# Two transformer blocks on one core: dues and lists of a hand-written planner (batch 0's output projections, the last pair of maxima, the outputs, the context pieces)

## The chip, the cores and the metric

One core of a Trainium2 chip runs the whole program in one launch. The time is the device's, in microseconds (us). The kernel before takes 2895.8 us (median of 3 runs, 2895.5 to 2897.63).

## What is computed

The reference applies two blocks (layers 0 and 1) to `x`, 4 batches of 512 tokens of width 320, with a context of 4 x 1601 tokens of width 192. Each block has three parts:

```python
h1 = _ln(x, n1_g, n1_b)
x = _attn(h1, h1, q1, k1, v1, o1_w, o1_b, 20) + x        # self
h2 = _ln(x, n2_g, n2_b)
x = _attn(h2, context, q2, k2, v2, o2_w, o2_b, 20) + x   # cross
h3 = _ln(x, n3_g, n3_b)
a, g = split(h3 @ ff_w1 + ff_b1)
x = a * gelu(g) @ ff_w2 + ff_b2 + x                      # feed-forward
```

`_attn` has 20 heads of 16 columns: `softmax(q k^T / 4) v`, then the output projection `@ wo + bo`.

## The kernel before

**Units.** Attention is done in units: one layer, one kind (self or cross), one batch `b` of 4, one group `g` of 4 heads out of 5 groups. A unit goes over its keys in chunks of 128: 4 chunks in self, 13 in cross. The program has 88 units in order: layer 0 self (units 0 to 19, batch by batch), layer 0 cross (20 to 39), four feed-forward units (40 to 43), and the same for layer 1 from unit 44.

**One chunk** (`main`, line 1323). TensorE works in strips of 32 rows, one per head, so four heads run beside each other. `score` (1330) makes for each head three passes into one bank: two of keys by queries (the queries are split in a rounded and a remaining half) and a third that adds the negative row maxima (`nrows`, line 1336). ScalarE takes the exponential (1346), TensorE multiplies by the values one chunk later (1362), ScalarE copies the product out (the first chunk into the unit's output `o`, line 1376; the others into `vo`, 1381), GpSimd adds (1382). `o` is a tile with two buffers (1375), so the unit after next needs the first one's place.

**Row maxima, ahead of time.** The next units' maxima are computed beside the present unit's scores: TensorE repeats the product with the queries as the stationary side (`sps`, 1088 and 1113), VectorE reduces each tile over the keys (1099, 1123). These products come as pairs for two heads each: 8 in a self unit, 26 in a cross unit, in two queues (`pairs[0]`, `pairs[1]`). A chunk has two half rounds, and each has one regular slot, which takes one pair from the queue of its parity; in it the maxima use the strips that the scores leave free. `giver` (line 1635) hands out the pairs of the next two units, and of the first cross unit (called early) from 9 units before. Besides the slots it can order extra rounds of up to two pairs, when pairs are owed by the pace that the remaining rounds ask for, or when a unit's pairs are left in its last slot (lines 1666 to 1671). A unit's pairs can be given 4 rounds after its queries and keys were sent (`at_hand`). When the present unit has two chunks left, `max_reduce` and `max_end` (1157, 1164) finish the next unit's maxima, turn them, and issue four small transfers to `nrows` (1183) from SP; the next unit's third passes wait for these.

**The planner.** Everything else is entered in lists (`chains`, line 396) by `add` with a cost in us of TensorE, a due half round, a condition that must hold (`ready`) and one before which it isn't tried (`soon`). A list is served only from its head. After each chunk `steps` (487) advances the round, adds credit by the pace that all dues ask for, and runs heads in the order of their due rounds (ties by the list's name); at the first one with a cost of 0.1 or more that the credit doesn't cover, it stops. Entries of cost LIGHT (0.01) are limited to one or two per chunk. `carry` (818) then issues the pending moves of queries and keys (888) and the errands.

**The way of an output** (`add_finish`, 1191). After a unit's last values, `turn` sends `o` to memory (1203), two rounds later at the earliest; the tile is then read back with another layout. After a batch's fifth unit: `sums` reads the denominators (1211), `invert` (1215), `save` (1220), `read` loads the first two thirds of the batch's output and of the inverse (1236, 1237), GpSimd multiplies them (`divide`, 1244), `load` fetches the last third a number of rounds later, `divide` again, and `end` (1271) enters eight output projections (`project`, 1255: 24 small products into `ops`, line 1262, and an addition on VectorE, 1269) and `done`, which marks the batch as ready for its next normalisation. `turn`, `invert`, `save`, the divisions and `end` of all units share the list "divide".

**The context, layer 0 only** (`add_turned`, 758). Each batch's context comes in 7 pieces (742, 748). VectorE transposes a piece into one of two `stages` buffers (767), SP saves it to memory (775). Batch 0's pieces are entered when unit 5 starts, with dues 2 rounds apart up to the 22nd round of the unit after; other batches' come in the cross stage, 6 apart. `add_context` reads the saved pieces back into the layout for the products (789), in two steps of four transfers.

**Banks.** The 8 PSUM banks are chosen by `bank` (413), which takes the one that is free first by `expect`, a running estimate of when each engine is done.

**The start** (from line 1695 on). The first units are prepared by an order written out by hand: two batches of `x` and the weights are loaded, units 0 to 3 projected, unit 0's maxima taken. While `start["on"]`, moves go to SP's and ScalarE's queues in turn (886), and so do the `nrows` transfers (1182).

Of the kernel before, what the change touches and what calls it, by code (L numbers as in the profile page):

```python
# [24 lines left out]
NQ = N // P  # L25
# [53 lines left out]
def kernel(ctx: ExitStack, tc: tile.TileContext, x, context, ws, out):  # L79
# [313 lines left out]

    chains = {n: deque() for n in ("divide", "project", "norm", "scale", "context", "early", "proj", "values")}
    clock = {"round": 0, "credit": 0.0, "lights": 0, "tiles": None, "ff": False, "cross": False}
    ALIKE = ("project", "early", "proj", "values")
    LIGHT = 0.01
# [440 lines left out]
    def add_proj(u):  # L840
# [35 lines left out]
        def move(of, pairs, may, gap=0):  # L876

            def f():
                pending[of] -= 1
                if of == "k":  # L880
                    room["sent"] = clock["round"]
                u.moving[of] = clock["round"]
                for to, src in pairs():
                    queue = nc.sync
                    if start["on"]:
                        queue = (nc.sync, nc.scalar)[room["first"] % 2]
                        room["first"] += 1
                    queue.dma_start(out=to.bitcast(F32), in_=src)
                u.open -= 1
                if not u.open:  # L890
                    u.when = -9 if start["on"] else clock["round"]

            pending[of] += 1
            u.moves[of].append((f, may, gap))
            u.moving[of] = clock["round"]
            if (u.i, of, u) not in movers:
                movers.append((u.i, of, u))
# [266 lines left out]
    def max_end(u):  # L1164

        top, high, low = (u.nm[:, :, i, :] for i in range(3))
        nc.vector.tensor_reduce(
            high.bitcast(F32R), top.rearrange("p j (t o) -> p j t o", o=1), AX.X, ALU.max, negate=True
        )
        nc.vector.tensor_reduce(  # L1170
            low, u.nm[:, :, 0:2, :].rearrange("p j e t -> p j t e"), AX.X, ALU.add, negate=True
        )
        turned = two.tile([P, SLOT], F32, tag="turned", name="turned")

        nc.vector.transpose(turned.rearrange("p (j c) -> p j c", j=HG), u.nm[:, :, 1:3, :].rearrange("p j e t -> p j (e t)"))
        busy("dve", 0.6)
        slots = u.rows.bitcast(F32).rearrange("(g s) n -> s g n", s=DH)[0].rearrange("g (t r) -> g t r", t=NQ)

        def rows():
            for i in range(P // SLOT):  # L1180
                part = slice(i * SLOT, (i + 1) * SLOT)
                queue = nc.scalar if start["on"] and i % 2 else nc.sync
                queue.dma_start(out=slots[:, :, part], in_=turned[part, :])

        if u.cross and u.before.cross:
            u.rows_of = rows
            errands.appendleft((clock["round"] + 1, yes, rows))
        else:
            rows()

    def add_finish(u):
# [34 lines left out]
        def read():  # L1226

            held["read"] += 1
            held["open"] += 1
            aT = one.tile([P, 3, N], F32, tag="aT", name="aT")  # L1230
            way, part = o_way[u.b % 2], {}

            def load(k, at, n):
                heads = slice(at // DH, (at + n) // DH)
                part[k] = two.tile([P, N], F32, tag="rT", name="rT")
                dma(out=aT[:n, k, :], in_=way[:DH, heads])
                dma(
                    out=part[k][:n],
                    in_=r_way[u.b % 2][heads].rearrange("(o j) n -> o j n", o=1).to_broadcast([DH, n // DH, N]),
                )  # L1240
                when.append(clock["round"])

            def divide(k, n):
                nc.gpsimd.tensor_tensor(aT[:n, k, :], aT[:n, k, :], part[k][:n], ALU.mult)  # L1244

            for k, at, n in DK[:2]:
                load(k, at, n)
            first, second, third = DK
            add("divide", 0.0, lambda: divide(0, first[2]), r - 20, yes, since(4, 3))
            add("divide", 0.0, lambda: divide(1, second[2]), r - 20)  # L1250
            add("divide", 0.0, lambda: load(*third), r - 20, yes, since(4, 5 if u.l and not u.cross else 7))
            add("divide", 0.0, lambda: divide(2, third[2]), r - 20, yes, since(5, 3))
            add("divide", 0.0, lambda: end(aT), r - 20)

# [15 lines left out]

        def end(aT):
            now = clock["round"]
            for t in range(NQ):
                for part in range(2):
                    add(
                        "project", (0.317,) * 3, lambda t=t, part=part: project(aT, t, part),
                        now + 2 + u.nch * t + u.nch // 2 * part, yes, lambda: clock["round"] >= now + 1,
                    )
            add("project", 0.0, done, now + 2 + u.nch * NQ)

        def done():
            held["open"] -= 1
            after(u)

        r = when[0]
        add("divide", 0.0, turn, r - 20, lambda: u.g or held["written"] < held["read"] + 2, since(0, 2))


    late = []
# [283 lines left out]
    def before(u):  # L1573

        if u.kind == "cross" and u.g == 1 and u.b + 1 < B or u.kind == "self" and u.m == EARLY - 3:
            b = u.b + 1 if u.cross else 0
            if u.l == 0:
                load_context(b, 0)
                load_context(b, 1)
                if u.cross:  # L1580
                    add_turned(b, u.start + 46, 6)
        if u.kind == "self" and u.m == 0 and u.l:
            take_rooms(u.l)
        if u.kind == "cross" and u.m == B * G - 1:
            take_weights()
            loads.extend(load_first(u.l, (0, 1, 3)) + load_ff(u.l)[2])
        if u.kind == "cross" and u.m == B * G - 3:
            take_rests()
            small, rests, _ = load_ff(u.l)
            loads.extend(small + rests)  # L1590
        if u.kind == "cross" and u.m == B * G - 2:
            loads.extend(load_first(u.l, (4, 2)))
        if u.kind == "self" and u.m == EARLY - 1 and u.l == 0:
            add_turned(0, units[u.i + 1].start + 22, 2)
        if u.kind == "self" and u.m == EARLY:

            add_context(0, lambda s: units[u.i - u.m + B * G].own.update(kv=s["cT"]), u.start + 36, yes)
# [37 lines left out]
    def giver(u):  # L1635
# [15 lines left out]
        def give(h, alone=False):  # L1651
# [7 lines left out]
            for v in coming:  # L1659
# [6 lines left out]
                rest = v.start - (7 if alone else 4) - clock["round"]  # L1666
                if rest > 0:
                    most = max(most, (total - rest * (not alone)) / (2 * rest))
                if left(v) and (rest == 1 or alone and rest < 1):
                    urgent = urgent or v  # L1670
                    owed = max(owed, 1.0 if alone and rest > -4 else (left(v) + 1) // 2)
            owed += most * went if total else 0.0
# [54 lines left out]
        run("norm")  # L1727
    max_reduce(first)
    max_end(first)
    at_once(units[2])  # L1730
    second = units[1]
    second.pairs = max_pairs(second)
    round_of(second.pairs[0].popleft()[1] + second.pairs[1].popleft()[1])
    add_proj(units[3])
    run("proj")
    run("proj")
    loads.extend(load_x(2))
    for fs in (load_out(0, "o1_w"), load_x(3), load_cross(0)):
        loads.extend(fs)
# [51 lines left out]
```

## Time and profile before

| | |
|---|---|
| median of 3 runs | 2895.8 us |
| the profiled execution, whole | 2899.26 us |
| its span, first to last instruction | 2897.2 us |
| mean granted TensorE clock | 0.997 |
| VectorE, ScalarE, GpSimd busy | 68%, 67%, 45% |
| HBM read and written | 55.76 and 29.36 MB |

The self stage of layer 0 ends at about 373 us of the span, that of layer 1 goes from about 1487 to 1808 us; between and after them lie the cross stages and, from about 1187 and 2622 us, the feed-forward stages.

How to read it: PE is TensorE's products, PEld its loading of weights, DVE is VectorE, ACT ScalarE, POOL GpSimd, SP SyncE, and a q behind a name is that engine's queue, where it waits or issues transfers. L1088 is line 1088 of the kernel. In the timeline a row has its start, its duration, engine, line, operation, output and inputs, and in brackets the engine's idle time before it with what ended it. In the table of windows a row has the stretch, its length, the busy time and number of instructions of PE, PEld, DVE, ACT and POOL, then the granted TensorE clock as a share of the full one, the busy share of the DMA engines, and GB/s. In the chain of waits a row has its start and duration on the path that ended last. Ends of products are modelled, so a TensorE that is shown as busy may still be held up.

### The profile page before, as it was taken

To read this page: it belongs to the slowest core of one execution; us is meant where nothing else is said; L and a number is where in the kernel's file an instruction comes from. 1 tells how busy PE (TensorE), PEld (TensorE's weight loads), DVE (VectorE), ACT (ScalarE), POOL (GpSimd) and SP (SyncE) were. 2 spreads that over 40 slices of the span, in tenths; PEclk is the share of its full clock that TensorE was granted. 3 is DMA by queue.
4 is the path that set the end of the run, shared out by engine and by line. 5 is a ranking of instruction groups with operands and counts; after the bars stand their busy time and mean duration, and the time that the engine had idled before them with its cause. 6 is when DMAs were issued, how large, how long until landed. Compare 5 with 4: busy or idle time off the path is not lost.

```text
span 2897.2 us, 83291 instructions
## 1 busy us (share of the span) xinstructions
PE 2848.3 (98%) x35028; PEld 1543.2 (53%) x35028; DVE 1972.1 (68%) x3734; ACT 1948.9 (67%) x4033; POOL 1307.5 (45%) x1420
## 2 busy tenths in 40 slices
PE   9999999999999999999999999999999999999999
PEld 5455555555555555355554555555555555544554
DVE  7867888788888888323257678888878878862221
ACT  4867678888888888501138776788888888893000
POOL 5556345555545546211225653455565564551100
PEclk9999999999999999999999999999999999999999
DMA  4444233232232112200123432221221122122000
GB/s 115 118 111 110 66 82 88 57 93 59 57 87 70 48 50 63 85 18 16 38 52 88 106 91 66 71 69 44 54 73 47 44 72 61 45 72 61 23 22 12
DMA packets 163502, 188.59 MB, mean 65 GB/s; under 512 B 62004, under 2 KB 109112, under 8 KB 163128
## 3 DMA queue, kind: packets, MB, share of 16 engines
q1 hardware_dynamic: 161464, 180.38, 24.5%
q8 instruction: 275, 4.51, 0.6%
q10 hardware_dynamic: 1664, 2.89, 0.4%
q14 instruction: 99, 0.81, 0.1%
HBM read 55.76 MB, written 29.36 MB: 29 GB/s over the span
## 4 chain that ended last, share of the span: by engine, by line
PE 87%; DVE 6%; POOL 3%; DMA 2%; issue 1%; ACT 1%; SPq 0%; POOLq 0%; ACTq 0%; DVEq 0%
PE av L1362 22%; PE st L1336 20%; PE fps L1447 10%; PE sps L1088 8%; PE yps L1554 6%; PE vps L1047 5%; PE ops L1262 4%; PE kps L984 3%; DVE nmax L1099 3%; PE qkps L920 3%; PE fps L1507 3%; PE qps L959 2%; DVE pm L1099 2%; PE sps L1113 1%; POOL hturned L630 1%
## 5 line engine op out<-in xcount | busy, mean ns | idle before, releaser
L1346 ACT ACTIVATE pr<-st 128x512 f32<-128x512 f32 (+1 forms) x2720 | 1404.8, 604 | 309.8 <-PE st L1336 278.2
L1099 DVE TENSOR_REDUCE pm<-sps 128x1 f32<-128x512 f32 (+1 forms) x1920 | 1149.1, 661 | 235.1 <-PE sps L1088 230.2
L1382 POOL TENSOR_TENSOR o<-o,vo 128x512 f32<-128x512 f32 x576 | 739.7, 1284 | 916.6 <-ACT vo L1381 899.0
L1088 PE MATMUL sps<-kT,q 32*128 32x512 f32 (+1 forms) x4800 | 858.2, 419 | 3.8 <-ACT halves L936 1.4
L1336 PE MATMUL st<-q,kT 32*128 32x512 f32 (+1 forms) x5120 | 785.3, 419 | 2.7 <-ACT o L1376 2.1
L1362 PE MATMUL av<-pr,vals 128*32 128x512 f32 (+1 forms) x5440 | 735.1, 606 | 30.9 <-ACT pr L1346 5.6
L1336 PEld LDWEIGHTS st<-q,kT 32*128 32x128 f32 (+1 forms) x5120 | 447.6, 180 | 284.1 <-issue 113.4
L1336 PE MATMUL st<-nrows,ones 32*128 32x512 f32 (+1 forms) x2720 | 560.5, 398 | 0.9 <-DMA nrows<-turned 0.7
L1099 DVE TENSOR_REDUCE nmax<-sps 128x1 f32<-128x512 f32 x640 | 397.0, 683 | 115.2 <-PE sps L1088 113.1
L1088 PEld LDWEIGHTS sps<-kT,q 32*128 32x128 f32 x4800 | 429.9, 183 | 54.7 <-ACT pr L1346 11.2
L1381 ACT COPY vo<-av 128x512 f32<-128x512 f32 x576 | 354.0, 615 | 17.4 <-PE av L1362 10.4
L1518 ACT ACTIVATE gl<-fps,b 128x512 f32<-128x512 f32 x80 | 54.7, 687 | 408.9 <-PE fps L1507 299.1
L1447 PE MATMUL fps<-hT,w 128*128 128x512 f32 x640 | 283.1, 597 | 0.0
L1362 PEld LDWEIGHTS av<-pr,vals 128*32 128x32 f32 (+1 forms) x5440 | 111.1, 108 | 304.2 <-DVE pm L1099 186.7
L1336 PEld LDWEIGHTS st<-nrows,ones 32*128 32x128 f32 (+1 forms) x2720 | 262.9, 180 | 10.1 <-issue 2.0
L1519 DVE SCALAR_TENSOR_TENSOR hid<-fps,b,gl 128x512 f32<-128x512 f32 x80 | 59.7, 748 | 249.2 <-ACT gl L1518 247.1
L1447 PEld LDWEIGHTS fps<-hT,w 128*128 128x128 f32 x640 | 119.3, 190 | 155.0 <-issue 151.6
L1554 PE MATMUL yps<-w,hid 128*128 128x320 f32 x640 | 175.7, 435 | 0.0
L1554 PEld LDWEIGHTS yps<-w,hid 128*128 128x128 f32 x640 | 120.6, 190 | 56.2 <-ACT gl L1518 5.3
L1262 PEld LDWEIGHTS ops<-wo,aT 112*32 112x32 f32 (+1 forms) x3072 | 98.9, 110 | 66.0 <-issue 34.9
L1262 PE MATMUL ops<-wo,aT 112*32 112x160 f32 (+1 forms) x3072 | 125.7, 301 | 2.6 <-POOL aT L1244 2.6
L1123 DVE TENSOR_REDUCE pm<-sps 128x4 f32<-128x508 f32 x160 | 99.0, 682 | 39.8 <-PE sps L1113 38.8
(89 smaller groups left out, 2458.2 us busy)
## 6 DMA issues: line engine op xcount, KB each, us to landing
kT<-stages SPq DMA_DIRECT2D x80, 400.5 KB
oway<-o SPq DMA_DIRECT2D x80, 256.0 KB
q<-halves SPq DMA_DIRECT2D x80, 256.0 KB
q<-halves SPq DMA_DIRECT2D x27, 512.0 KB
kT<-halves SPq DMA_DIRECT2D x40, 256.0 KB
aT<-oway SPq DMA_DIRECT2D x32, 224.0 KB
rT<-rway SPq DMA_DIRECT2D x32, 224.0 KB
hT<-hturned SPq DMA_DIRECT2D x96, 64.0 KB
```

The costliest lines, as they stand in the source:

```text
L1047: nc.tensor.matmul(ps[f : f + m, :w], lhsT=u.kvT[:n, k, at + f : at + f + m], rhs=wv[:n, k, h0 * DH : h1 * DH], start=(k == 0), stop=(k == ...
L1088: nc.tensor.matmul(own[0][:, :w], lhsT=u.queries(slice(j * SLOT, (j + 1) * SLOT), e, t), rhs=u.kT[j * SLOT : (j + 1) * SLOT, u.k0 + at : u ...
L1099: nc.vector.tensor_reduce(to, own[0][:, :w], AX.X, ALU.max)
L1123: nc.vector.tensor_reduce(u.pm[:, :, j, ns - 1], ps[:, : NQ * w].rearrange("p (t w) -> p t w", w=w)[:, :, :n], AX.X, ALU.max,)
L1262: nc.tensor.matmul(ps[f : f + m, : D // 2], lhsT=aT[:n, k, f * NQ + t * SLOT : f * NQ + t * SLOT + m], rhs=wo[:n, k, cols], start=(k == 0) ...
L1336: nc.tensor.matmul(own[0][:r, :], lhsT=ones[rows, :r] if e == 2 else u.keys(rows, c), rhs=u.rows[rows, :] if e == 2 else u.queries(rows, e ...
L1346: nc.scalar.activation(p[:r], own[0][:r], AF.Exp)
L1362: nc.tensor.matmul(ps[j * SLOT : (j + 1) * SLOT, :], lhsT=columns_of[:r, head : head + SLOT], rhs=pr.pop((c, j))[:r, :], start=True, stop= ...
L1381: nc.scalar.copy(vo, ps)
L1382: nc.gpsimd.tensor_tensor(u.o, u.o, vo, ALU.add)
L1447: nc.tensor.matmul(ps, lhsT=w1[:, k, i * FF + c * P : i * FF + (c + 1) * P], rhs=natural(u.hT[:, k]), start=start, stop=stop,)
L1554: nc.tensor.matmul(ps[:, :D], lhsT=hid[c][:, t * P : (t + 1) * P], rhs=w2[:, c, :], start=(c == 0), stop=(c == NHC - 1),)
```

## The change

- The list "way" is new and holds the `turn` of each unit; "divide" keeps the rest.
- The last third of a batch's output is loaded 5 rounds after the second in both layers' self stages, where layer 0 had 7.
- `end`: the projections of batch 0's self output are due one round apart instead of two (self units have `nch` 4), and `done` accordingly; other batches and the cross stage keep their spacing.
- `giver`: one pair left in a unit's last slot, if it belongs to the queue of that slot, no longer counts as urgent, and so is given in the slot and not in an extra round.
- Batch 0's context pieces are due 3 rounds apart instead of 2, up to the same last round.
- In the start, `at_once(units[2])`, which issues unit 2's moves of queries and keys, stands behind unit 1's first maxima and unit 3's projections; and `expect` counts ScalarE's time for the transfers that it issues.

```diff
-    chains = {n: deque() for n in ("divide", "project", "norm", "scale", "context", "early", "proj", "values")}
+    chains = {n: deque() for n in ("way", "divide", "project", "norm", "scale", "context", "early", "proj", "values")}
...
                         queue = (nc.sync, nc.scalar)[room["first"] % 2]
                         room["first"] += 1
                     queue.dma_start(out=to.bitcast(F32), in_=src)
+                    if queue is nc.scalar:
+                        expect["act"] += 0.6
...
                 queue = nc.scalar if start["on"] and i % 2 else nc.sync
                 queue.dma_start(out=slots[:, :, part], in_=turned[part, :])
+                if queue is nc.scalar:
+                    expect["act"] = max(expect["act"], expect["dve"]) + 1.05
...
-            add("divide", 0.0, lambda: load(*third), r - 20, yes, since(4, 5 if u.l and not u.cross else 7))
+            add("divide", 0.0, lambda: load(*third), r - 20, yes, since(4, 7 if u.cross else 5))
...
         def end(aT):
             now = clock["round"]
+            apart = 1 if not u.cross and u.b == 0 else u.nch // 2
             for t in range(NQ):
                 for part in range(2):
                     add(
                         "project", (0.317,) * 3, lambda t=t, part=part: project(aT, t, part),
-                        now + 2 + u.nch * t + u.nch // 2 * part, yes, lambda: clock["round"] >= now + 1,
+                        now + 2 + u.nch * t + u.nch // 2 * part if u.cross else now + 2 + apart * (2 * t + part), yes, lambda: clock["round"] >= now + 1,
                     )
-            add("project", 0.0, done, now + 2 + u.nch * NQ)
+            add("project", 0.0, done, now + 2 + (u.nch * NQ if u.cross else 2 * NQ * apart))
...
-        add("divide", 0.0, turn, r - 20, lambda: u.g or held["written"] < held["read"] + 2, since(0, 2))
+        add("way", 0.0, turn, r - 20, lambda: u.g or held["written"] < held["read"] + 2, since(0, 2))
...
         if u.kind == "self" and u.m == EARLY - 1 and u.l == 0:
-            add_turned(0, units[u.i + 1].start + 22, 2)
+            add_turned(0, units[u.i + 1].start + 22, 3)
...
-                if left(v) and (rest == 1 or alone and rest < 1):
+                if left(v) > bool(not alone and v.pairs[h % 2]) and (rest == 1 or alone and rest < 1):
                     urgent = urgent or v
...
     max_reduce(first)
     max_end(first)
-    at_once(units[2])
     second = units[1]
     second.pairs = max_pairs(second)
     round_of(second.pairs[0].popleft()[1] + second.pairs[1].popleft()[1])
     add_proj(units[3])
     run("proj")
     run("proj")
+    at_once(units[2])
```

## The prediction

> **What bounds the kernel now.** I read the page first: share of each engine and the chain that ended last.
>
> ```profile
> span 2897.2 us, 83291 instructions
> PE 2848.3 (98%) x35028; PEld 1543.2 (53%) x35028; DVE 1972.1 (68%) x3734; ACT 1948.9 (67%) x4033; POOL 1307.5 (45%) x1420
> ...
> PE 87%; DVE 6%; POOL 3%; DMA 2%; issue 1%; ACT 1%; SPq 0%; POOLq 0%; ACTq 0%; DVEq 0%
> ```
>
> TensorE is the bound: idle for 2897.2 - 2848.3 = 48.9 us. The change alters neither the arithmetic nor the number of matrix products, so it can win only what TensorE loses in waits and in rounds that fill the array badly. Where that is, the two layers tell: their self stages do the same work, but layer 0 also turns the context (L767, L775). I cut both stages by batch (the window view; first column the stretch and its length): batches 1, 2, 3 of layer 0, then of layer 1.
>
> ```profile
> 117.90:201.50 83.60, 77.98 (x1124) 41.48 (x1125) 62.01 (x128) 58.83 (x119) 47.19 (x58) 0.98 0.51 133
> 201.50:290.30 88.80, 85.56 (x1276) 47.49 (x1276) 59.98 (x118) 62.05 (x129) 53.90 (x65) 0.98 0.37 93
> 290.30:373.20 82.90, 81.06 (x1164) 44.56 (x1160) 68.66 (x131) 56.63 (x117) 26.71 (x23) 0.98 0.23 61
> 1563.00:1641.40 78.40, 75.41 (x1125) 41.21 (x1125) 58.35 (x115) 58.74 (x119) 47.06 (x58) 1.00 0.41 107
> 1641.40:1726.40 85.00, 83.42 (x1299) 47.00 (x1291) 59.44 (x118) 62.41 (x129) 53.87 (x65) 1.00 0.38 97
> 1726.40:1808.10 81.70, 79.92 (x1165) 44.60 (x1166) 69.40 (x133) 56.31 (x117) 26.77 (x22) 1.00 0.24 62
> ```
>
> With nearly the same products, layer 0 is longer by 5.2, 3.8 and 1.2 us. Batch 2 first, in the timeline:
>
> ```profile
> 254.92 1.28 POOL L1382 TENSOR_TENSOR o<-o,vo 128x512 f32<-128x512 f32 x1 [0.70 <-ACT vo L1381]
> ...
> 264.90 0.78 SPq L1203 DMA_DIRECT2D oway<-o  x1
> ...
> 271.24 0.57 SPq L1203 DMA_DIRECT2D oway<-o  x1
> ...
> 275.23 0.58 ACT L1376 COPY o<-av 128x512 f32<-128x512 f32 x1 [4.68 <-DMA oway<-o]
> ...
> 275.87 0.73 PE L1336 MATMUL st<-q,kT 32*128 32x512 f32 x3 [2.08 <-ACT o L1376]
> ```
>
> The third unit's output is complete at 256.2 but leaves at 264.90, 6.3 us before the next unit's. What holds it is the list: `turn` is entered in "divide", only the head of a list is ever run, and at the head stand batch 1's divisions, which wait a set number of rounds for their loads. The output buffer has two places, so ScalarE's copy two units on waits 4.68 us for that transfer, and TensorE 2.08 us for ScalarE. In batch 1:
>
> ```profile
> 157.98 0.98 SPq L775 DMA_DIRECT2D ctxT<-stages  x1
> ...
> 163.51 0.60 SPq L775 DMA_DIRECT2D ctxT<-stages  x1
> ...
> 167.42 1.28 POOL L1382 TENSOR_TENSOR o<-o,vo 128x512 f32<-128x512 f32 x1
> ...
> 170.66 0.38 DVE L767 STREAM_TRANSPOSE stages<-stages 128x192 f32<-128x192 f32 x1 [3.25 <-DMA ctxT<-stages]
> ...
> 171.62 2.67 SPq L1183 DMA_DIRECT2D nrows<-turned  x4
> ...
> 172.19 1.94 PE L1362 MATMUL av<-pr,vals 128*32 128x512 f32 x8 [2.44 <-DVE nmax L1099]
> ...
> 179.31 0.60 SPq L1203 DMA_DIRECT2D oway<-o  x1
> ```
>
> The seventh context piece is turned in the buffer of the fifth, whose save left one chunk earlier (163.51). VectorE waits 3.25 us for it, the maxima stand behind it, TensorE stands 2.44 us. After both stops it runs slowly; behind the five engines' busy times stands the granted clock, 0.53 and 0.75:
>
> ```profile
> 172.00:175.00 3.00, 2.81 (x20) 0.99 (x24) 1.93 (x4) 0.58 (x1) 1.19 (x3) 0.53 0.04 8
> 276.00:280.00 4.00, 4.00 (x45) 2.31 (x49) 1.29 (x2) 3.09 (x7) 2.66 (x3) 0.75 0.23 69
> ```
>
> So a stop costs more than its idle time, and the difference between the layers, not the gap, is the price to use.
>
> **Outputs in their own list.** Of the turns, only those are held that fall behind a batch's pending divisions: by the rounds of `add_finish`, one per batch 0, 1 and 2 in each layer. In layer 0 the worst is batch 2's third unit: ready in round 108 (three after its last values), issued in 114 with `end`. Now it goes in 108, soon after 256.2. What is late next there: batch 1's aT loads and the row maxima on SP, which layer 1 has too; its batch 2 takes 85.00. I take **-3.5 us** of the 3.8 (range 0 to -4.7, the copy's wait). Layer 1's held turns were late by two to four rounds and stop nothing in its stretches: nothing.
>
> **Context pieces apart.** The same seven turnings and saves; only their due rounds move, from 56, 58, ... 68 to 49, 52, ... 67. Entries run when at the head and no dearer work is due before them, so the first pieces come up to six rounds sooner and the fifth piece's save takes the place of the row at 157.98, whose successor did not wait. The 3.25 us wait should go. But the last save and the first reading of the saved context move too, from round 70 to 68, and with the output now in 68 instead of 72 three things stand on SP ahead of unit 9's row maxima: an output that waits for GpSimd until 167.42 + 1.28 = 168.7, the save, and four reads that wait for the save to land:
>
> ```profile
> 163.51 7.03 DMA ctxT<-stages
> ...
> 174.34 2.29 DMA ctxT<-stages
> ...
> 331.63 3.01 DMA nrows<-turned
> ```
>
> The reads and, in the window view, the fourth unit of batch 1 in layers 0 and 1:
>
> ```profile
> 176.68 2.53 SPq L789 DMA_DIRECT2D w<-ctxT  x4
> ```
>
> ```profile
> 161.80:179.70 17.90, 14.99 (x187) 6.97 (x179) 11.39 (x23) 11.39 (x24) 15.43 (x24) 0.90 0.51 119
> 1605.90:1621.80 15.90, 14.27 (x213) 7.50 (x213) 10.77 (x21) 11.33 (x24) 15.32 (x24) 1.00 0.55 146
> ```
>
> From 168.7: output 0.6, save landed 2.9 later (2.29, and some more for the output ahead of it), reads 2.53, row maxima 2.67 to issue and 3.01 to land: 168.7 + 0.6 + 2.9 + 2.5 + 2.7 + 3.0 = 180.4. At layer 1's pace TensorE is at unit 9 by 161.8 + 15.9 = 177.7: a new wait of 2.7, and some half microsecond of slow clock behind it. So of 5.2 us I take **-2.0 us**; ends -5.2 (the reads find the save landed) and +2 (7.03 instead of 2.9 for the save, 5.2 - 2.7 - 4.1 - 0.5). The Trainium skill, "DMA: Bandwidth & Descriptors", section "Queues, rings and completion order", says that a transfer's semaphore lands only after every earlier write of the same DMA engines; by it the save always waits for the 256 KB output ahead of it. The rows 7.03 and 2.29 fit that; were it the 7.03 every time, the term would be +2 and the sum -5.0.
>
> **The last pair of maxima.** A pair left over in the last slot was forced into a round of its own. An extra round, in layer 0's batch 3:
>
> ```profile
> 324.66 0.76 PE L1088 MATMUL sps<-kT,q 32*128 32x512 f32 x8
> 325.46 2.42 DVE L1099 TENSOR_REDUCE pm<-sps 128x1 f32<-128x512 f32 x4 [0.24 <-PE sps L1088]
> ```
>
> Four tiles cost 0.76 us where TensorE decides, 2.42 where VectorE does. By the giver's rule the condition holds three times in a layer: at the first unit and the first cross unit it spent a full extra round on the unit after next; before the first cross unit it took that unit's very last pair alone, two tiles. The lone round goes: half of 0.76 to 2.42, so 0.4 to 1.2, I take 0.8, twice: 1.6. The full ones only move: that pair is given in a later slot or extra round, out of places where VectorE is behind; four times 0.3, between 0 and 2.42 - 0.76 = 1.7 each: 1.2. Nothing waits longer: VectorE reduces in order, so `max_reduce` came behind as many reductions before.
>
> **Batch 0's projections.** Eight at one round instead of two:
>
> ```profile
> 291.88 0.82 PE ops L1262 x24
> 1620.37 0.48 PE L1262 MATMUL ops<-wo,aT 96*32 96x160 f32 x8 [1.36 <-POOL aT L1244]
> 182.71 2.12 PE L1262 MATMUL ops<-wo,aT 96*32 96x160 f32 x56 [0.64 <-POOL aT L1244]
> ```
>
> 8 x 0.82 = 6.6 us of TensorE move, none is added. The batch is done some six rounds sooner, and the first cross unit's normalisation, queries and 26 pairs may start so much sooner; its extra rounds spread over longer. Twice 0.35: 0.7 (0 to 2.4, one full extra per layer). With the lone and moved rounds **-3.5 us** (0 to -10). The third aT load two rounds earlier in layer 0 makes it like layer 1, where the first projection meets GpSimd's division: 1.36 instead of 0.64, **+0.7 us** (0 to +1.4).
>
> **The start.**
>
> ```profile
> 36.04 0.60 ACTq L888 DMA_DIRECT2D q<-halves  x1
> 36.77 0.84 ACT L936 ACTIVATE halves<-qkps,scales 128x256 f32<-128x256 f32 x2 [4.13 <-POOL x L623]
> 37.29 0.50 PE L1088 MATMUL sps<-kT,q 32*128 32x512 f32 x2 [1.37 <-ACT halves L936]
> ```
>
> Unit 2's moves now stand behind unit 3's projections, so ScalarE copies before it issues, and the added ScalarE times choose banks that are free. TensorE's 1.37 us goes at most; the row maxima's transfer, issued by 36.0, is late next. **-0.7 us** (0 to -1.4).
>
> **Sum.** -3.5 - 2.0 - 3.5 + 0.7 - 0.7 = -9.0 us. The profiled execution took 2899.3 us (span 2897.2 and 2.1 around it): 2890.3. It is 3.5 above the median 2895.8, the difference of two executions of one program; against the median: **2886.8 us**. The measurement can tell 0.2%, 5.8 us: 2890.0 and 2901.6 are the limits.
>
> **The rivals.** *The stops only change places* (29%): the new wait on SP is 5.5 instead of 2.7 (batch 1 then 5.5 + 0.5 - 5.2 = +0.8), the moved and lone extra rounds yield 1.0, the start 0.5: -3.5 + 0.8 - 1.0 + 0.7 - 0.5 = -3.5, 2892.3. For it: SP is in order and the chain of batch 1 is full of it. In it lies too that the change does not do what it says where the output waits for GpSimd anyway; against that the 254.92 row.
>
> *Slower* (11%): outputs at the head of SP hold up the row maxima.
>
> ```profile
> SPq L1203 <- POOL o L1382: 334.2, 67, 10.6
> ```
>
> SP already stands 334.2 / 67 = 5.0 us on average at an output. Moved forward, six of them (three per layer) come ahead of a unit's row maxima; if each makes those 2.7 us late, as worked out above, and nothing of batches 1 and 2 is won: 6 x 2.7 - 3.5 + 0.7 - 0.7 = +12.7, so 2908.5. It decides once the maxima land after the next unit's third pass, some two chunks after issue. Against it, from the costliest groups (last column: TensorE's idle time before the third passes):
>
> ```profile
> L1336 PE MATMUL st<-nrows,ones 32*128 32x512 f32 (+1 forms) x2720 | 560.5, 398 | 0.9 <-DMA nrows<-turned 0.7
> ```
>
> Today 0.9 us are lost there in 80 units, 74 of which already send their output at once.
>
> *Only the gaps count* (5%): the Trainium skill, "TensorE: Matmul & The Clock Gate", section "Part 1: The HAM clock gate", puts the slow clock behind an idle window of about 3.4 us, longer than either gap. As a mechanism of this kernel: the 2.08 and 2.44 us gaps would be all that a removed stop gives, 2.1 in batch 2 and 2.44 x 2.0 / 5.2 = 0.9 in batch 1: -2.1 - 0.9 - 3.5 + 0.7 - 0.7 = -6.5, 2889.3. The rows with 0.53 and 0.75 speak against it.
>
> **Numbers.** The forecast has 55%, its own range 2880 to 2890. Chances: faster 0.55 + 0.05 = 0.60, same 0.29, slower 0.11. Range: the forecast's far end, -4.7 - 5.2 - 5 (half of the extra rounds' bound) - 0.7, is 2880; upwards it takes in the rival of changed places and its neighbours to 2897.
>
> **What would show it.** Right: batch 2 of layer 0 near 85 us, no copy waiting on the output's transfer; no transposition waiting on a save; the same counts at L1088 and L1099. A wait of TensorE for row maxima of about 2.7 us at the last unit of batch 1 shows the new order on SP; of 5.5, the first rival. Wrong: batches 1 and 2 of layer 0 as long as before, or waits for row maxima in layer 1 as well.

## The result and the profile after

The changed kernel takes 2886.18 us (median of 8 runs), the kernel before, beside it on the same chip, 2895.65 us (median of 8): the ratio is 0.9971, 95% interval 0.9962 to 0.9979. The medians are 9.5 us apart; by the ratio the gain is 8.4 us, between 6 and 11.

First the page: span and busy times, and from the costliest groups the third passes, whose last column is TensorE's idle time before them.

```profile
span 2884.7 us, 83201 instructions
PE 2833.2 (98%) x35028; PEld 1539.2 (53%) x35028; DVE 1975.2 (68%) x3734; ACT 1948.6 (68%) x4033; POOL 1307.5 (45%) x1420
...
L1341 PE MATMUL st<-nrows,ones 32*128 32x512 f32 (+1 forms) x2720 | 561.5, 398 | 8.3 <-DMA nrows<-turned 8.2
```

The counts are those of before, as they should be. TensorE's idle time has not fallen (2884.7 - 2833.2 = 51.5 us, before 48.9): the whole gain lies in time in which TensorE counted as busy and was held up or ran at a lower clock (the mean granted clock of the two traces is 0.999 and 0.997). And one idle stop is new: 8.2 us for row maxima where there were 0.7.

Where it went is in the windows, cut at the starts of the same units as before (stretch, length, busy times, granted clock, DMA share, GB/s). In order: unit 0, batches 1 and 2 of layer 0's self stage, its first cross unit, unit 44 (layer 1's first), layer 1's batch 1.

```profile
37.70:55.00 17.30, 17.10 (x260) 9.25 (x256) 12.01 (x22) 12.09 (x25) 6.03 (x6) 1.00 0.61 156
112.90:201.30 88.40, 79.60 (x1176) 43.18 (x1177) 63.35 (x132) 59.70 (x120) 47.54 (x59) 0.96 0.49 124
201.30:285.60 84.30, 82.77 (x1259) 46.39 (x1256) 61.63 (x119) 61.58 (x128) 53.03 (x65) 1.00 0.38 95
365.70:410.50 44.80, 44.18 (x676) 25.22 (x672) 35.81 (x65) 36.42 (x79) 21.41 (x18) 1.00 0.26 71
1478.30:1492.80 14.50, 14.04 (x160) 7.19 (x161) 11.70 (x23) 10.85 (x21) 5.21 (x6) 1.00 0.45 110
1550.90:1630.60 79.70, 76.45 (x1151) 42.18 (x1148) 59.40 (x118) 59.32 (x119) 47.40 (x59) 1.00 0.39 103
```

The three that the prediction did not show, in the kernel before (unit 0, first cross unit, unit 44):

```profile
38.10:60.00 21.90, 21.49 (x270) 11.29 (x266) 15.35 (x28) 12.67 (x26) 6.22 (x7) 0.92 0.45 116
373.20:421.20 48.00, 47.68 (x736) 27.36 (x731) 38.01 (x69) 37.28 (x81) 23.35 (x21) 1.00 0.26 68
1487.30:1505.20 17.90, 17.39 (x167) 8.65 (x169) 14.17 (x27) 11.33 (x22) 5.24 (x6) 0.90 0.41 99
```

Batch 2 of layer 0 went from 88.8 to 84.3, as forecast. Batch 1 went the wrong way, 83.6 to 88.4. The first units gave 4.6 and 3.4 us, the first cross unit of layer 0 gave 3.2: much more than the prediction had for them, though part of the 4.6 and 3.4 is the slow clock of the trace of before (0.92 and 0.90). In batch 2 the timeline of the changed kernel shows the mechanism that was meant: the third unit's output is complete at 254.5, leaves at 256.41, and the copy two units on waits for nothing.

```profile
253.24 1.28 POOL L1387 TENSOR_TENSOR o<-o,vo 128x512 f32<-128x512 f32 x1 [1.43 <-ACT vo L1386]
...
256.41 0.60 SPq L1207 DMA_DIRECT2D oway<-o  x1
...
274.73 0.62 ACT L1381 COPY o<-av 128x512 f32<-128x512 f32 x1
```

Batch 1's stop, in the timeline and then in the chain of waits (start, duration, what):

```profile
163.90 0.59 SPq L1207 DMA_DIRECT2D oway<-o  x1
164.58 0.54 SPq L775 DMA_DIRECT2D ctxT<-stages  x1
170.47 3.98 SPq L789 DMA_DIRECT2D w<-ctxT  x4
174.56 2.66 SPq L1185 DMA_DIRECT2D nrows<-turned  x4
...
178.53 0.79 PE L1341 MATMUL st<-nrows,ones 32*128 32x512 f32 x2 [5.84 <-DMA nrows<-turned]
```

```profile
164.58 5.84 DMA ctxT<-stages
...
176.64 1.64 DMA nrows<-turned
```

Nothing waits for a save to free its buffer any more. Instead output, save and reads stand ahead of unit 9's row maxima on SP, the reads until the save has landed, 5.84 us after its issue. TensorE stands for 5.84 us too (the equal figures are chance), and then runs for 6 us at half to three quarters of its clock:

```profile
178.50:181.50 3.00, 2.98 (x20) 1.29 (x24) 1.22 (x2) 2.07 (x4) 0.00 (x0) 0.50 0.81 211
181.50:184.50 3.00, 3.00 (x64) 2.19 (x60) 0.49 (x3) 0.59 (x1) 1.27 (x1) 0.71 0.90 247
```

### The profile page after: what moved, and what is told of

Read it like the earlier page. It is cut to its first block, busy times and chain, and to the rows that moved or that the text cites. A ratio compares the mean times of both kernels' runs of the same rounds, so it can differ in the third digit from the quotient of the medians.

```text
span 2884.7 us, 83201 instructions
## 1 busy us (share of the span) xinstructions
PE 2833.2 (98%) x35028; PEld 1539.2 (53%) x35028; DVE 1975.2 (68%) x3734; ACT 1948.6 (68%) x4033; POOL 1307.5 (45%) x1420
## 4 chain that ended last, share of the span: by engine, by line
PE 87%; DVE 8%; POOL 1%; issue 1%; DMA 1%; ACT 1%; SPq 1%; ACTq 0%; POOLq 0%; DVEq 0%
PE av L1367 22%; PE st L1341 20%; PE fps L1452 10%; PE sps L1090 9%; PE yps L1559 6%; PE vps L1049 5%; PE ops L1266 4%; DVE nmax L1101 3%; PE kps L986 3%; PE qkps L922 3%; PE fps L1512 3%; PE qps L961 2%; DVE pm L1101 2%; DVE pm L1125 2%; PE sps L1115 1%
## 5 line engine op out<-in xcount | busy, mean ns | idle before, releaser
L1090 PE MATMUL sps<-kT,q 32*128 32x450 f32 (+1 forms) x4800 | 858.1, 419 | 2.3 <-ACT vo L1386 1.2
```

Source lines behind the costliest of these rows:

```text
L1090: nc.tensor.matmul(own[0][:, :w], lhsT=u.queries(slice(j * SLOT, (j + 1) * SLOT), e, t), rhs=u.kT[j * SLOT : (j + 1) * SLOT, u.k0 + at : u ...
```

## Experiments

The theory after this look: a full extra round that is taken out of a first unit is worth all that VectorE needs for it; the outputs' list does what was forecast; the context pieces' new dues cost time, because the reads go ahead of the row maxima. Rivals: the projections earn the cross units' share, the start earns unit 0's, the output ahead on SP makes the stop.

| kernel | us | ratio to before | 95% interval |
|---|---|---|---|
| the change | 2886.18 | 0.9971 | 0.9962 to 0.9979 |
| giver's line alone | 2890.93 | 0.9984 | 0.9975 to 0.9993 |
| batch 0's projections and third load alone | 2893.22 | 0.9995 | 0.9986 to 1.0004 |
| outputs' list alone | 2893.28 | 0.9990 | 0.9981 to 0.9999 |
| context pieces alone | 2894.95 | 1.0001 | 0.9992 to 1.0009 |
| start alone | 2891.76 | 0.9996 | 0.9987 to 1.0005 |
| third load alone | 2896.73 | 1.0008 | 0.9999 to 1.0017 |
| change without the giver's line | 2892.79 | 0.9997 | 0.9988 to 1.0006 |
| change without the context's dues | 2882.67 | 0.9963 | 0.9950 to 0.9975 |
| **change with later reads** | **2878.61** | **0.9951** | 0.9938 to 0.9965 |
| later reads, outputs in the old list | 2880.46 | 0.9955 | 0.9941 to 0.9968 |
| later reads, later projections | 2882.25 | 0.9959 | 0.9946 to 0.9971 |

The ratios are to runs of the kernel before on the same chip, whose medians went from 2893.5 to 2895.65; so kernels are compared by ratio, and places by their traces. The first five rows "alone" (without the third load alone, which the second of them contains) make up the change and multiply to 0.9966, near the change's 0.9971.

**The kernel before, once more.** No edit. It comes first, since it says how far the other traces can be read.

> The kernel before, unchanged, profiled once more. If the stops of its trace are fixed by the program: the same waits (3.25 us for the save, 4.68 us for the output) within some tenths, and the same granted clock in unit 0 and unit 44. If their size is that of one execution: the waits stand at the same places with other lengths (1.9 and 3.0 us, as in traces of kernels with the same order there), some of the stretches of slow clock are gone, and the span is 3 to 9 us shorter than 2897.2.

The span is 2891.3, 5.9 shorter than the trace that the prediction was made from. Windows of unit 0, batch 1, batch 2 and unit 44, then rows of the timeline, TensorE's gap before unit 0 first, its wait behind the held-up output of batch 2 last:

```profile
38.20:58.40 20.20, 19.78 (x270) 10.38 (x266) 15.27 (x28) 12.54 (x25) 6.16 (x7) 1.00 0.48 126
116.30:198.50 82.20, 76.05 (x1124) 41.08 (x1125) 62.12 (x128) 59.00 (x120) 47.14 (x58) 1.00 0.52 135
198.50:285.30 86.80, 83.76 (x1276) 46.55 (x1272) 59.92 (x118) 61.87 (x128) 53.91 (x65) 1.00 0.38 95
1480.80:1499.60 18.80, 18.38 (x166) 9.54 (x169) 14.12 (x27) 11.26 (x22) 5.21 (x6) 0.82 0.39 94
```

```profile
37.37 0.50 PE L1088 MATMUL sps<-kT,q 32*128 32x512 f32 x2 [1.38 <-ACT halves L936]
...
167.75 0.38 DVE L767 STREAM_TRANSPOSE stages<-stages 128x192 f32<-128x192 f32 x1 [1.86 <-DMA ctxT<-stages]
...
169.28 1.06 PE L1362 MATMUL av<-pr,vals 128*32 128x512 f32 x8 [1.40 <-DVE nmax L1099]
...
179.33 2.12 PE L1262 MATMUL ops<-wo,aT 96*32 96x160 f32 x56 [1.84 <-POOL aT L1244]
...
272.57 0.73 PE L1336 MATMUL st<-q,kT 32*128 32x512 f32 x3 [1.83 <-ACT o L1376]
```

The stops stand at the same places. That of the output is nearly as long as before: ScalarE's copy waits 4.41 us instead of 4.68, TensorE 1.83 instead of 2.08. The size of the other is that of one execution: 1.86 us for the save instead of 3.25, and TensorE 1.40 instead of 2.44. What TensorE saved there it lost 10 us later, waiting for GpSimd's division: 1.84 instead of 0.64. The two together are 3.08 and 3.24. In unit 0 the slow clock is gone (20.2 us instead of 21.9), in unit 44 it is worse (0.82). A difference under 2 us at these places, between one trace and one other, says nothing by itself.

**The giver's line alone, and the change without it.**

```diff
-                if left(v) and (rest == 1 or alone and rest < 1):
+                if left(v) > bool(not alone and v.pairs[h % 2]) and (rest == 1 or alone and rest < 1):
```

> The kernel before with the giver's line alone (one pair left in its own slot is not urgent). By the prediction's terms: the lone rounds 2 x 0.8 and four full rounds moved at 0.3, so 2.8 us faster. By the theory that the trace after suggests (a round taken out is worth what VectorE takes for it, 2.4 us, and some slow clock behind): the first units of both layers 3 to 4 us shorter each, the first cross units 1 to 3, the last self units 1.5 each, in all 10 to 14 us faster. By the rival that the shorter cross units come from batch 0's earlier projections: 6 to 8 us faster, all of it in the first units.

> The kernel after with the giver's old line. If a full round taken out is worth VectorE's 2.4 us and more: 10 to 14 us slower than the changed kernel, that is slower than the kernel before by up to 3. By the prediction's terms: 2.8 us slower than the changed kernel, 2889.

Unit 0 with the line alone:

```profile
38.30:55.90 17.60, 17.39 (x262) 9.45 (x258) 13.13 (x24) 12.13 (x26) 6.19 (x7) 1.00 0.56 145
```

and unit 0, the first cross unit and unit 44 in the change without it:

```profile
37.80:57.70 19.90, 19.54 (x268) 10.22 (x264) 14.93 (x28) 12.52 (x25) 6.13 (x7) 1.00 0.50 129
367.70:413.60 45.90, 45.64 (x684) 25.91 (x680) 37.56 (x68) 36.73 (x79) 21.00 (x18) 1.00 0.26 69
1481.40:1498.30 16.90, 16.40 (x166) 8.01 (x169) 14.05 (x27) 11.29 (x21) 5.22 (x6) 1.00 0.43 105
```

Between these rows and those of the change, all at full clock, a full extra round in a first unit is worth 19.9 - 17.3 = 2.6 and 16.9 - 14.5 = 2.4 us, as much as VectorE's four reductions take (2.42). In the first cross unit it is worth 45.9 - 44.8 = 1.1. VectorE's column confirms it: 14.93 us (28 instructions) against 12.01 (22) in unit 0; the pair is reduced in a later slot, and the rest of batch 0 is no longer for that (57.9 us with and without). The measured whole is smaller than 10 to 14 us: 0.16% alone, and 0.26% in the change (0.9971 / 0.9997), some 4.6 and 7.5 us; the expectation of 14 had taken in what the second trace of before shows to be one execution's. Nor do the places add up to the whole: a round that is taken out at one place can come back at another. With the line alone VectorE has 135 instructions in batch 3, four more than in the second trace of before, and batch 3 takes 81.9 us instead of 81.4. In the change it also has four more than without the line (131 and 127), but there that costs nothing (80.1 and 80.2 us).

**Batch 0's projections with the third load; the third load alone.** The second is the first line, the first has the change's `end` with `apart` as well.

```diff
-            add("divide", 0.0, lambda: load(*third), r - 20, yes, since(4, 5 if u.l and not u.cross else 7))
+            add("divide", 0.0, lambda: load(*third), r - 20, yes, since(4, 7 if u.cross else 5))
...
+            apart = 1 if not u.cross and u.b == 0 else u.nch // 2
```

> The kernel before with batch 0's projections one round apart and the third load after 5 rounds in both layers. By the prediction's terms -0.7 + 0.7 = nothing, within 1 us. By the rival that the shorter first cross units belong to these projections: 3 to 5 us faster, seen in units 20 and 64 and the last self units.

> The kernel before with the third load of batch outputs after 5 rounds in both layers, alone. By the prediction's term 0.7 us slower. If this line alone already ends the held-up output of batch 2 (the divisions end one chunk sooner, and the output behind them leaves sooner): no copy waits for the output's transfer, batch 2 of layer 0 near 84 to 85, 3 to 4 us below the profiled execution of before, and the first projection's wait for GpSimd within 0.5 of before's 0.64.

Batches 1 and 2 and the first cross unit with both:

```profile
118.10:203.80 85.70, 78.59 (x1176) 42.94 (x1177) 63.17 (x132) 59.66 (x121) 47.77 (x59) 0.98 0.50 128
203.80:287.90 84.10, 82.63 (x1256) 46.16 (x1252) 61.06 (x119) 61.48 (x127) 52.86 (x65) 1.00 0.37 95
368.20:414.90 46.70, 45.84 (x684) 25.93 (x683) 38.35 (x69) 36.76 (x79) 21.71 (x19) 1.00 0.27 73
```

The same three with the third load alone, and its stop in batch 1:

```profile
116.30:203.80 87.50, 79.42 (x1148) 42.62 (x1149) 62.34 (x129) 58.99 (x119) 47.14 (x58) 0.96 0.49 126
203.80:289.30 85.50, 82.50 (x1275) 45.85 (x1271) 60.25 (x118) 62.24 (x129) 54.02 (x65) 1.00 0.38 97
370.60:417.50 46.90, 45.82 (x684) 25.95 (x680) 38.48 (x69) 36.74 (x80) 21.96 (x19) 1.00 0.28 74
```

```profile
169.78 0.38 DVE L767 STREAM_TRANSPOSE stages<-stages 128x192 f32<-128x192 f32 x1 [3.92 <-DMA ctxT<-stages]
```

This was not expected by the prediction: with the divisions done one chunk sooner, the outputs behind them in the list leave sooner too, no copy in the stage waits for an output's transfer, and batch 2's stop is gone without a list of its own (85.5 us, where the traces of before have 88.8 and 86.8). In batch 1 the load goes to SP ahead of the context's saves, VectorE waits 3.92 us and TensorE 3.44, and batch 1 (87.5 against 83.6 and 82.2) gives back what batch 2 gains or more: the whole is the same or slower.

The rival on the projections is not borne out where it looked: the first cross unit of layer 0 is 46.7 instead of 48.0 and 47.9 in the two traces of before, but 46.9 with the third load alone, and in layer 1 there is no such gain. The projections do earn something: batches 1 and 2 together take 169.8 us with both edits and 173.0 with the load alone, and the ratios 0.9995 and 1.0008 are 0.13% apart, some 3.8 us. The intervals of the two overlap, and why the batches gain is open.

**The outputs' list alone, and without it beside later reads** (for which see below).

```diff
-        add("divide", 0.0, turn, r - 20, lambda: u.g or held["written"] < held["read"] + 2, since(0, 2))
+        add("way", 0.0, turn, r - 20, lambda: u.g or held["written"] < held["read"] + 2, since(0, 2))
```

> The kernel before with the outputs' own list alone. By the prediction 3.5 us faster, all of it in batch 2 of layer 0 (88.8 to about 85), nothing in batch 1 and in layer 1. By the rival (outputs ahead on SP hold up row maxima): batch 1 of layer 0 longer by 1 us or more, with a wait for row maxima at the last unit's first chunk, and the whole the same as before.

> The changed kernel with the later reads (label read4) and with the outputs back in the list of the divisions. If the earlier third load alone cures batch 2: within 1 us of read4, 2878 to 2880, batch 2 of layer 0 the same 84. If the outputs' own list is needed for it, as the prediction had it: batch 2 longer by about 3.5 us, 2882.

Batch 2 with the list alone; then with the outputs in the old list, but all else of the change and later reads:

```profile
201.30:285.40 84.10, 82.84 (x1276) 46.28 (x1272) 59.76 (x118) 62.10 (x128) 53.91 (x65) 1.00 0.39 99
```

```profile
193.40:277.60 84.20, 82.72 (x1256) 46.21 (x1252) 61.53 (x119) 61.50 (x128) 52.87 (x65) 1.00 0.37 95
```

The list alone does cure batch 2 (84.1), and in part it does what the rival said: in batch 1 TensorE waits 1.03 us for unit 9's row maxima, which go out behind the output and a save, and batch 1 takes 84.4 us where the second trace of before has 82.2. The whole is still faster, by 0.1%. In the change it does what the third load does anyway: by the traces the kernel without it is the same in every stretch (84.2 and 84.2 in batch 2, spans 2876.9 and 2876.8). The medians lie 1.9 us apart, with intervals that overlap.

**The context pieces: alone, undone, and with later reads.** The first edit alone, the change with it undone, and the change with the second:

```diff
-            add_turned(0, units[u.i + 1].start + 22, 2)
+            add_turned(0, units[u.i + 1].start + 22, 3)
...
-            add_context(0, lambda s: units[u.i - u.m + B * G].own.update(kv=s["cT"]), u.start + 36, yes)
+            add_context(0, lambda s: units[u.i - u.m + B * G].own.update(kv=s["cT"]), u.start + 40, yes)
```

> The kernel before with the context pieces 3 rounds apart alone, so that the third output still leaves with unit 9's first chunk and only the last save and the first reads stand ahead of unit 9's row maxima. If the reads are what holds up the row maxima: the save lands 2.3 us after its issue, reads 2.5, maxima 2.7 and 3.0, and TensorE still waits 2 to 4 us there; batch 1 of layer 0 81 to 83 us, 1 to 3 us faster. If it takes the output ahead of the save to make a wait: no wait there, batch 1 near 78.4, 5 us faster.

> The kernel after with the context pieces 2 rounds apart again. If the pieces' new dues are what made batch 1 of layer 0 longer (88.4 where it was 83.6): batch 1 back to about 83.6, so 4 to 5 us faster than the changed kernel, some 2881.5. If the output ahead on SP did it: batch 1 stays near 88 and the time near 2886.

> The kernel after with the first reading of the saved context due 4 rounds later, so that it goes to SP behind unit 9's row maxima and one chunk behind the save. If the reads standing ahead, waiting for the save, cost the 5.84 us: the wait goes, and the slow clock with it, batch 1 of layer 0 near layer 1's 79.7 to 81, 7 to 9 us faster than the changed kernel, near 2878. If the output and the save by themselves hold up the maxima: a wait of 2 us or more stays and the time falls by under 4.

(By the edit the last piece's due moves a round too, from 68 to 67.) The pieces' dues alone, in batch 1: the window, and TensorE's two waits there.

```profile
117.90:199.90 82.00, 76.80 (x1127) 41.38 (x1125) 61.97 (x128) 59.15 (x120) 47.03 (x58) 0.98 0.54 135
```

```profile
175.66 0.50 PE L1336 MATMUL st<-nrows,ones 32*128 32x512 f32 x2 [0.62 <-issue]
...
180.81 2.77 PE L1262 MATMUL ops<-wo,aT 96*32 96x160 f32 x56 [2.63 <-POOL aT L1244]
```

Neither theory had this. VectorE's wait is gone, TensorE stands 0.62 us before the third passes (the profile names nothing that it waited for), and then the first projection waits 2.63 us for GpSimd: 3.25 in all, as in both traces of before (3.08, 3.24). Batch 1 takes 82.0 where the second trace of before has 82.2, and the first projection starts 62.9 us after the batch does, there 63.0. The stop that was removed had covered the next one: as the division ends no sooner, nothing ahead of it earns anything.

In the change without the new dues:

```profile
113.00:197.00 84.00, 78.20 (x1176) 42.79 (x1177) 63.19 (x132) 59.73 (x120) 47.69 (x59) 0.98 0.51 131
```

```profile
167.88 1.93 PE L1367 MATMUL av<-pr,vals 128*32 128x512 f32 x8 [3.37 <-DVE nmax L1101]
```

and with the new dues and the reads later:

```profile
113.00:193.60 80.60, 77.33 (x1176) 42.19 (x1177) 63.26 (x132) 59.55 (x120) 47.56 (x59) 1.00 0.54 136
```

```profile
164.33 0.60 SPq L1207 DMA_DIRECT2D oway<-o  x1
165.02 0.54 SPq L775 DMA_DIRECT2D ctxT<-stages  x1
165.66 3.75 SPq L1185 DMA_DIRECT2D nrows<-turned  x4
...
170.97 2.73 SPq L789 DMA_DIRECT2D w<-ctxT  x4
171.15 1.30 PE L1266 MATMUL ops<-wo,aT 96*32 96x160 f32 x32 [0.84 <-POOL aT L1248]
```

The output and the save stand where they stood; the reads alone moved, the row maxima go out at 165.66 instead of 174.56, and TensorE's waits in this place are 0.84 us in all instead of 0.81 + 5.84. Batch 1 falls from 88.4 to 80.6, at full clock. So the reads ahead of the maxima made the stop, not the output. With them out of the way, the pieces' dues are worth 84.0 - 80.6 = 3.4 us. This kernel beats both, in five runs each (none above 2880.6 us, none of the change without the new dues below 2882.1): 0.9951 of before, 14 us.

**The start alone.** The three edits of the change's diff: `at_once(units[2])` behind the projections, and the two additions to `expect["act"]`.

> The kernel before with the start's changes alone (unit 2's moves later, ScalarE's issuing counted). By the prediction 0.7 us faster, in front of and in unit 0; at most 1.4. If the start carries the 4.6 us that unit 0 lost: 4 us faster, all of it before 60 us.

Unit 0 begins at 37.7 instead of 38.1 and 38.2 in the two traces of before, and takes 19.9 us where the second has 20.2: 0.7 to 0.8 in all, as forecast. The 2 us against the first trace are its slow clock.

**Later projections.** The change with later reads, and batch 0's projections of the self output tried three rounds after `end` instead of one.

```diff
-... lambda: clock["round"] >= now + 1,
+... lambda: clock["round"] >= now + (3 if not u.cross and u.b == 0 else 1),
```

> The changed kernel with the later reads, and with the projections of batch 0's self output tried two rounds later, so that GpSimd's division is done by then. If the waits of 0.84 and 1.35 us at the first projections are on the path: 1 to 2 us faster than read4, 2877. If what is late next takes their place, or the extra rounds that move with it cost as much: within 1 us of read4.

The two waits for GpSimd are gone (batch 1 at 79.5 instead of 80.6), and the whole is no faster (0.9959 against 0.9951, with intervals that overlap). Its trace is 1.6 us longer than that of the kernel with later reads: unit 44 ran with a clock of 0.89, and in layer 1 TensorE waits 1.77 us for row maxima in batch 2. The slow clock may well belong to the edit: in unit 44 the granted clock is 1.00 in all six traces of kernels that have the projections as in the change, and 0.82 to 0.91 in the other eight, this one among them. By what way is open.

## Why the prediction was right, and where not

The total was right within 0.6 us of the median, and most of the mechanisms were. Two parts were off in opposite directions by nearly the same: batch 1 came out 5.5 to 6.9 us dearer than its term (the projections that moved into it taken off), the rounds that were taken out some 6 us better than theirs. So the fit of the sum is partly luck. It was also read from a trace whose span is 5.9 us longer than that of another execution of the same kernel.

**Outputs, -3.5:** right. Batch 2 lost 4.5 us against the first trace of before and 2.5 against the second. Missed: the third load's earlier round does the same. The two were costed as separate, and they overlap.

**Third load, +0.7:** the price was looked for at the wrong place. The first projection's wait is 0.81, much as before (0.64). What the line really does is to move a load ahead of the saves and the division forward by a chunk: alone it costs batch 1 a stop of 3.9 us on VectorE and ends that of batch 2, and the whole is 0.08% slower (-0.01% to 0.17%). Without it the pieces' dues paid nothing, with it and the later reads 3.4 us; that it is the load that makes the difference is argued from the division's earlier end, not run by itself.

**Context pieces, -2.0:** wrong in sign. Batch 1 grew by 4.8 and 6.2 us against the two traces of before; some 1.3 of it, as in layer 1 (78.4 to 79.7), are projections that now fall into it (1176 products instead of 1124). The place was right. The step that failed is the sum "168.7 + 0.6 + 2.9 + 2.5 + 2.7 + 3.0 = 180.4": from the output's issue to the landing of the maxima it counts 11.7 us, measured were 178.28 - 163.90 = 14.4, because the save landed after 5.84 and not 2.9, and the reads took 3.98 and not 2.53 (the maxima's landing, 1.64 instead of 3.0, gave some of it back). TensorE stood at unit 9 by 172.7, 8.8 us after the output's issue, where 177.7 - 168.7 = 9.0 was forecast. So the wait is 5.84 instead of 2.7, the first rival's 5.5. And "some half microsecond of slow clock" was 3 x 0.50 + 3 x 0.29 = 2.4 us. Both ends of the save's price, 2.29 and 7.03, had been quoted; the likelier was taken for the one nearest in time, although an output went ahead of the save in the new order and none in the row of 2.29. (Nor in the row of 7.03, which has a context load and two moves ahead of it.) The rule of the Trainium skill cited in the prediction ("DMA: Bandwidth & Descriptors", section "Queues, rings and completion order": the semaphore lands only after the earlier writes of the same engines) pointed to the dear end. The runs do not single it out: with an output just ahead the save took 5.84, and with the pieces' dues alone, no output ahead but a load, the reads began 169.28 - 164.98 = 4.3 us after its issue.

**The value of the stop, 5.2 us (batch 1 of layer 0 against layer 1):** a layer's difference had been taken for the price of one stop. The runs show a second stop under it, GpSimd's division, that would have taken the gain alone.

**Last pair and projections, -3.5:** too small. The rounds of the last self units are worth some 0.8 each, as taken. The four moved full rounds were put at 0.3 each "between 0 and 2.42 - 0.76 = 1.7"; they are worth 2.6, 2.4, 1.1 and 1.1 by the traces with and without the line, 7.2 instead of 1.2 (the whole shows less, as said above: 4.6 us for the line alone and 7.5 in the change, with the rounds of the last self units in them). The bound itself failed: the reason given was that the pair "is given in a later slot or extra round, out of places where VectorE is behind", with TensorE's 0.76 still to be paid there. In a slot the pair uses strips that the scores leave free, so the whole round goes. The projections' 0.7 was placed in the first cross units, where the runs show 0.2 in layer 0 (46.9 to 46.7) and nothing in layer 1; what they earn, some 3.8 us by the ratios, lies elsewhere.

**Start, -0.7:** right, 0.4 to 0.5 ahead of unit 0 and 0.3 in it.

**Rivals.** "The stops only change places" is what happened in batch 1, stop and size; it did not decide, since the extra rounds yielded some seven times what that rival gave them. "Outputs hold up row maxima" came with the list alone, in one place and by 1.03 us. In the change it did not: SP stands at an output 73 times instead of 67, the six forecast, but the only long wait for row maxima is the one in batch 1, and the later reads cure it with the output left in front.

```profile
SPq L1207 <- POOL o L1387: 357.5, 73, 10.6
```

"Only the gaps count" has the rows of 0.53 and 0.75 in the first trace of before against it, and batch 2's 4.5 us; in the second trace, where the clock stayed at 1.00 behind the gaps of 1.40 and 1.83 us, batch 2 lost 2.5 us to the change, near the 2.1 of that rival. That TensorE's idle time rose while the time fell does not decide it, since most of the gain is from the extra rounds.

## What to carry to other kernels

On an in-order queue a transfer that waits for another must not stand ahead of one that the bound engine needs: ask of each entry not how long it takes but what it waits for, and put a chunk of other work between a save and its reading. A stop that is removed is worth only what the next one behind it leaves, which a comparison with another stage doesn't show; look for the second wait before pricing the first. And profile the kernel before twice: a stop's place is the program's, its length may be one execution's.

## What the hardware showed that was not expected

The granted clock fell in one execution and not in another after the same gap. Before unit 0 the kernel before has a gap of 1.37 us in one trace and 1.38 in the other (both quoted above); the window from 38 to 43 us, first in the first trace, then in the second:

```profile
38.00:43.00 5.00, 4.97 (x70) 2.96 (x66) 2.48 (x4) 2.71 (x6) 1.55 (x2) 0.66 1.01 248
```

```profile
38.00:43.00 5.00, 4.87 (x90) 2.85 (x82) 3.75 (x7) 3.65 (x9) 1.63 (x2) 1.00 0.99 247
```

It costs 1.7 us of unit 0. Of all traces six have this gap of 1.37 to 1.40 us, all without the start's edits; three of them have the slow clock behind it. None of the eight others has the slow clock in unit 0.

The Trainium skill, "TensorE: Matmul & The Clock Gate", section "Part 1: The HAM clock gate", says that the window over which activity is counted runs freely, so that it depends on the phase where the clock changes; this agrees with the two rows. It puts the slow clock behind an idle window of about 3.4 us; here gaps of 1.37 and 2.44 us had it behind them, and gaps of 1.40 and 1.83 (at 169.28 and 272.57 in the second trace, whose batches 1 and 2 ran at 1.00) had not.
